# Attention scores spread over partitions by DMA transposes of 16-bit halves instead of TensorE transposes

## The chip, the cores and the metric

The kernel runs on one core of a Trainium2 chip. The metric is the device time of one execution in microseconds (us), lower is better. The engines are named as the profile names them: PE is the matrix engine (TensorE), PEld its weight loads, DVE the vector engine, ACT the scalar engine, POOL is GpSimd, SP the engine that issues DMAs.

## The reference, cut to what matters

There are 128 graphs of 128 nodes with 256 features, each with its own 128x128 matrix of edges. Layer 0 is a gated graph network: three rounds, each of which sums messages over the edges and puts them through a gated recurrent cell. Layer 1 is an attention over the edges, and this is where the change lies:

```python
h = jnp.maximum(_layernorm(x, axis=-1), 0.0)
Wh = jnp.einsum('bnf,fo->bno', h, W)
s = Wh.sum(axis=-1)
e = jax.nn.leaky_relu(s[:, :, None] + s[:, None, :], negative_slope=ALPHA)
e = jnp.where(adj == 0, -jnp.inf, e)
alpha = jax.nn.softmax(e, axis=-1)
h_prime = jnp.einsum('bpq,bqo->bpo', alpha, Wh)
x = x + h_prime
```

The score s is one number for each node. The sum `s[:, :, None] + s[:, None, :]` needs it twice: once by row and once by column.

## The kernel before, in words

The 128 graphs are worked on in 32 groups of four (`G`). A group's tiles hold the nodes of a graph on the 128 partitions, or its features, with the four graphs side by side.

Each group goes through three rounds of the gated cell (`gru` twice, then `gru_rows`, which leaves the nodes on the partitions) and then through `attention`. Rounds of different groups alternate: in the steady part the order is round 0 of group g, round 1 of g-1, round 2 of g-2, and so on (`turns`). One such round is a slot.

The gate products of a round (`products`, L663 and L670 in the profile) are made with a seven-product scheme, and their banks of PSUM, the matrix engine's output memory, are `x`, `y` and `q`, each in a part for two gates (`_rz`) and one for the third (`_n`). After its sixth product the `y` bank is copied to SBUF by ACT (`put`, L702 and L706) and then added to by the seventh product. PE's next products for `y_rz` must therefore wait for that copy; the products for `y_n` lie between. The remaining PE work of a group is: edge sums (L605), weighted sums of attention (L619), rows products of attention (L966), and the transposes of the scores (L923). They share two PSUM banks named `misc`.

The order of all instructions on every engine is written out by a planner, the class `Plan`. Every operation is given to it with an engine, a length in ns, and the buffers that it reads and writes. `run` plays the engines forward in time, with lags between engines (`LAG`: 250 to 300 ns, 4000 for a DMA), and at each step takes among the operations that can start first the one with the earliest rank. A rank is a due time less the lengths of what follows. The gate products are a chain of fixed order, one behind the other. Whatever feeds them is ranked earlier by `MARGIN`, which is 8000 ns before and 7000 after. Each engine then runs its list strictly in that order and waits on semaphores.

In `attention` (L891) the rows x1 are normalised to h1 (`normed`), of which there is one buffer. Then:

- Four DVE operations (L899) multiply h1 by the column sums of W and add up each row: the scores s, one column for each of the four graphs, a node on each partition.
- L917 makes e, which is 0 on edges and a huge negative number elsewhere.
- L923 spreads s over the partitions: for each graph, one column of s is read as a 128x128 tile (the column repeated 128 times) and PE transposes that. The result in `misc` has s of all nodes along the free dimension on every partition.
- L929 adds it to e, L930 adds s by row, L932 applies the leaky slope, L934 and L936 find the row maximum, L941 takes the exponential on ACT. The exponential is held back by `turn` until a given copy of a later group's round 1 has been made.
- e is transposed to eT. In all groups but the last two, `turned_weights` (L978) does this by DMA. A DMA transpose takes 16-bit elements, so ACT first splits e into a plane of low and one of high halves (`pe`, L985), SP issues one DMA transpose (L986) to `peT`, and ACT joins the halves again (L989). In the last two groups PE transposes e (L953) and ACT copies it (L955).
- `weighted` (L611) multiplies h1 by eT, L966 multiplies the result by W, L971 divides by the row sums and adds to x1, and x1 goes out.

The same DMA route by halves serves the states of the gated cell (`turned_halves`, L544 for the split, L554 for the DMA, L548 for the join).

Buffers are counted in the table `BUFS`. pe, peT, eT and h1 have one buffer, e and s two, `misc` two.

Of the kernel before, what the change touches and what calls it, by code (L numbers as in the profile page):

```python
# [11 lines left out]
U16 = mybir.dt.uint16  # L12
AF = mybir.ActivationFunctionType
OP = mybir.AluOpType
AX = mybir.AxisListType

P = 128
G = 4
# [2 lines left out]
SETS = 4  # L21
EARLY = 3
SLOT = 18150
MARGIN = 8000
GATES = 18150
BIG = 3.0e38

# [9 lines left out]
class Plan:  # L37
# [14 lines left out]
    def buf(self, tag):  # L52
        n, kind = self.tags[tag]
        if kind == "free" or kind == "turn":
            b = Buf(tag, tag, None)
            if kind == "turn":
                self.waiting.setdefault(tag, []).append((self.phase, len(self.waiting.get(tag, ())), b))
            return b
        key = (tag, self.group % SETS if kind == "set" else 0)
        uses = self.last.setdefault(key, [])  # L60
        b = Buf(tag, key, uses[-n] if len(uses) >= n else None)
        b.slot = (key[1], len(uses) % n)
        uses.append(b)
        return b
# [39 lines left out]
    def run(self):  # L104
# [29 lines left out]
        def rank_all():  # L134
            for i in reversed(topo):
                eng, ns, due = nodes[i][0], nodes[i][1], nodes[i][5]
                gap = 0 if i in bound else MARGIN
                rank[i] = min([due] + [rank[u] - (0 if nodes[u][0] == eng != "SP" else nodes[i][7])
# [72 lines left out]
def kernel(  # L211
# [21 lines left out]
    nc = tc.nc  # L233
    B, N, D = x.shape
    L = weight.shape[0]
    KD = D // P
    NG = B // G
# [5 lines left out]
    work = ctx.enter_context(tc.tile_pool(name="work", bufs=1))  # L243
# [5 lines left out]
        "at": (1, "all", work, [P, G, N]), "a": (6, "all", work, [P, G, N]),  # L249
        "hT": (1, "set", work, [P, KD, GN]), "rows": (3, "turn", work, [P, G, D]),  # L250
        "pl": (1, "turn", work, [P, 2, 3, GN]), "plT": (1, "turn", work, [P, 2, 3, GN]),
        "pe": (1, "all", work, [P, 2, G * N]), "peT": (1, "all", work, [P, 2, G * N]),
        "r1": (1, "turn", work, [P, G, D]), "p3": (1, "turn", work, [P, G, D]),
        "hs": (2, "turn", work, [P, 4, H]), "aT": (2, "turn", work, [P, KD, GN]),
        "gs": (2, "turn", work, [P, 4, H]),
# [35 lines left out]
    def ap(b):  # L291
        return phys[(b.tag,) + b.slot]

    plan = Plan({t: v[:2] for t, v in BUFS.items()})
    op, buf = plan.op, plan.buf

    ident = const.tile([P, P], F32, name="ident")
# [210 lines left out]
    def flat(b):  # L508
        return ap(b).rearrange("p q n -> p (q n)")
# [101 lines left out]
    def weighted(m, a, dst, lo, hi):  # L611

        n, cols = hi - lo, slice(lo * N, hi * N)
        for k in range(KD):
            ps = buf("misc")

            def sums(k=k, ps=ps):
                for b in range(lo, hi):
                    nc.tensor.matmul(flat(ps)[:, b * N:(b + 1) * N],  # L619
                                     ap(m)[:, b, k * P:(k + 1) * P], ap(a)[:, b, :],  # L620
                                     start=True, stop=True)
            op("PE", 225 * n, sums, [(m, lo, hi), (a, lo, hi)], [ps], [dst])
            units = (dst, 2 * k, 2 * k + 2) if n == G else (dst, 2 * k + lo // 2, 2 * k + hi // 2)
            op("ACT", 190 + 100 * n, lambda k=k, ps=ps: nc.scalar.copy(  # L624
                ap(dst)[:, k, cols], flat(ps)[:, cols]), [ps], [units])
# [224 lines left out]
    def group(g):  # L850
# [37 lines left out]
        for lo, hi in ((0, G),) if g < NG - 1 else ((G // 2, G), (0, G // 2)):  # L888
            attention(g, a, x1, h1, lo, hi)

    def attention(g, a, x1, h1, lo, hi):  # L891

        part, n = slice(lo, hi), hi - lo
        w1, w1_sum = W["w1"], W["w1_sum"]
        normed(x1, h1, lo, hi)
        s = buf("s")
        for b in range(lo, hi):
            hw = buf("hw")
            op("DVE", 520, lambda b=b, hw=hw: nc.vector.scalar_tensor_tensor(  # L899
                ap(hw), ap(h1)[:, b, :], 1.0, ap(w1_sum), op0=OP.mult, op1=OP.mult,  # L900
                accum_out=ap(s)[:, b:b + 1]), [(h1, b, b + 1), w1_sum], [hw, (s, b, b + 1)],
               two=True)

        e, top, low, den, rden = (buf(t) for t in ("e", "top", "low", "den", "rden"))

        def wide(t):
            return ap(t)[:, part, None].to_broadcast([P, n, N])

        def es():
            return ap(e)[:, part]

        def small(t):
            return ap(t)[:, part]
        cost = 155 + 134 * n
        op("DVE", 150 + 66 * n, lambda: nc.vector.tensor_scalar(  # L917
            es(), ap(a)[:, part], 0.0, -BIG, op0=OP.is_equal, op1=OP.mult), [(a, lo, hi)], [e])
        s_all = buf("misc")

        def turn_s():
            for b in range(lo, hi):
                nc.tensor.transpose(flat(s_all)[:, b * N:(b + 1) * N],  # L923
                                    ap(s)[:, b:b + 1].to_broadcast([P, P]), ident)

        def spread():
            return flat(s_all)[:, lo * N:hi * N].rearrange("p (b n) -> p b n", n=N)
        op("PE", 110 * n, turn_s, [s], [s_all], [e])
        op("DVE", cost, lambda: nc.vector.tensor_tensor(es(), es(), spread(), OP.add), [s_all], [e])  # L929
        op("DVE", cost, lambda: nc.vector.tensor_tensor(es(), es(), wide(s), OP.add), [s], [e],  # L930
           two=True)
        op("DVE", cost, lambda: nc.vector.scalar_tensor_tensor(  # L932
            es(), es(), ALPHA, es(), op0=OP.mult, op1=OP.max), [], [e], two=True)
        op("DVE", cost, lambda: nc.vector.tensor_reduce(small(top), es(), AX.X, OP.max),  # L934
           [e], [top])
        op("DVE", 150, lambda: nc.vector.tensor_scalar(  # L936
            small(low), small(top), -BIG / 1e3, -1.0, op0=OP.max, op1=OP.mult), [top], [low])

        def exps():
            for b in range(lo, hi):  # L940
                nc.scalar.activation(ap(e)[:, b, :], ap(e)[:, b, :], AF.Exp, bias=ap(low)[:, b:b + 1])  # L941
        op("ACT", 320 * n, exps, [low], [e], turn=(g + 2, 1, "rz"))
        op("DVE", cost, lambda: nc.vector.tensor_reduce(small(den), es(), AX.X, OP.add), [e], [den])
        op("DVE", 170, lambda: nc.vector.reciprocal(small(rden), small(den)), [den], [rden])
        eT, uT = buf("eT"), buf("uT")
        if g < NG - 2:
            turned_weights(e, eT)
        else:
            p_e = buf("misc")

            def turn():
                for b in range(lo, hi):
                    nc.tensor.transpose(flat(p_e)[:, b * N:(b + 1) * N], ap(e)[:, b, :], ident)  # L953
            op("PE", 110 * n, turn, [e], [p_e], [eT])
            op("ACT", 190 + 100 * n, lambda: nc.scalar.copy(  # L955
                ap(eT)[:, part].rearrange("p b n -> p (b n)"), flat(p_e)[:, lo * N:hi * N]),
               [p_e], [(eT, lo, hi)])

        weighted(h1, eT, uT, lo, hi)
        for m in range(lo, hi, 2):  # L960
            ps = buf("misc")

            def rows_product(m=m, ps=ps):
                for b in range(2):
                    for k in range(KD):
                        nc.tensor.matmul(ap(ps)[:, b, :], ap(uT)[:, k, (m + b) * N:(m + b + 1) * N],  # L966
                                         ap(w1)[:, k, :], start=(k == 0), stop=(k == KD - 1))
            op("PE", 4 * 432, rows_product,
               [(uT, m // 2, m // 2 + 1), (uT, 2 + m // 2, 3 + m // 2), w1], [ps])
            for b in range(2):  # L970
                op("DVE", 480, lambda b=b, i=m + b, ps=ps: nc.vector.scalar_tensor_tensor(  # L971
                    ap(x1)[:, i, :], ap(ps)[:, b, :], ap(rden)[:, i:i + 1], ap(x1)[:, i, :],
                    op0=OP.mult, op1=OP.add), [ps, rden], [(x1, m + b, m + b + 1)])
        op("SP", 100, lambda: nc.sync.dma_start(
            out[g * G + lo:g * G + hi].rearrange("b n d -> n b d"), ap(x1)[:, part]),
           [(x1, lo, hi)], [])

    def turned_weights(e, eT):  # L978

        pe, peT = buf("pe"), buf("peT")  # L980

        def halves(t):
            return ap(t).rearrange("p g n -> p (g n)").bitcast(U16).rearrange(
                "p (m two) -> p two m", two=2)
        op("ACT", 1045, lambda: nc.scalar.copy(ap(pe), halves(e)), [e], [pe])  # L985
        op("SP", 100, lambda: nc.sync.dma_start_transpose(  # L986
            ap(peT).rearrange("p two (g q) -> p (two g) q", q=P),
            ap(pe).rearrange("p two m -> p (two m)")), [pe], [peT])
        op("ACT", 1340, lambda: nc.scalar.copy(halves(eT), ap(peT)), [peT], [eT])  # L989

    weights()
    for g in range(NG):
# [33 lines left out]
```

## Time and profile before

The time is 2131.06 us, the median of three runs (2127.33 to 2132.03). The profiled execution spans 2129.0 us.

| engine | busy us | share |
|---|---|---|
| PE | 2108.4 | 99% |
| DVE | 1701.3 | 80% |
| ACT | 1536.5 | 72% |
| POOL | 923.8 | 43% |

| line | what | count | mean ns of one |
|---|---|---|---|
| L923 | PE transpose of s | 128 | 273 |
| L929 | DVE add of spread s, from PSUM | 31 of four graphs | 685 |
| L930 | DVE add of s by row, from SBUF | 31 of four graphs | 740 |
| L985 | ACT split of e | 30 | 1037 |
| L986 | DMA transpose pe to peT, issue to landing | 30 | 3.2 us |
| L989 | ACT join to eT | 30 | 1348 |
| L702 | ACT copies of gate banks | 448 | about 580 |

[...]What one adds to a full queue is seen from start to start. Idle time of an engine is put down to what released it. In the steady part the pattern repeats every two groups: the transposes of every second group start 129.20 us apart.

### The profile page before, as it was taken

Reading aid. Unit: us, or ns where it says so; the run is one execution under the profiler, and the core shown is the slowest. Engines: PE = TensorE matmul, PEld = TensorE weight load, DVE = VectorE, ACT = ScalarE, POOL = GpSimd, SP = SyncE. Lnnn points to the kernel's source line nnn. Section 1 sums busy time; section 2 is a strip of 40 time slices with the busy share of each in tenths; the row PEclk is TensorE's granted clock in tenths of the full one; section 3 lists DMA queues with packets and bytes.
Section 4 is the critical chain, followed back from the end, with each engine's and each line's share of the span. In section 5 each row is a group of like instructions: output and inputs, shape, how many; then the busy total and the mean of one; then the engine's idle time right before and its main releaser. Section 6 shows DMA issues by size and latency. Waiting matters only on the chain. (4 is left out here: it accounts for less than half of the span.)

```text
span 2129.0 us, 34073 instructions
## 1 busy us (share of the span) xinstructions
PE 2108.4 (99%) x12550; PEld 1882.8 (88%) x12550; DVE 1701.3 (80%) x3364; ACT 1536.5 (72%) x2771; POOL 923.8 (43%) x889
## 2 busy tenths in 40 slices
PE   8999999999999999999999999999999999999997
PEld 7888888898888998889998898998889988898896
DVE  7767898778787887877888787887878887877785
ACT  5567787767777676877767777677776777676663
POOL 5544454344543435434444443444434454434331
PEclk9999999999999999999999999999999999999997
DMA  4222223232222322323222322222223222212220
GB/s 144 45 50 50 48 51 72 50 65 54 64 67 55 79 56 50 68 58 80 45 60 58 75 67 50 65 56 64 66 55 75 60 50 70 60 31 53 58 75 30
DMA packets 333430, 129.35 MB, mean 61 GB/s; under 512 B 264656, under 2 KB 333008, under 8 KB 333264
## 3 DMA queue, kind: packets, MB, share of 16 engines
q1 hardware_dynamic: 333264, 127.18, 26.3%
q8 instruction: 98, 1.61, 0.3%
q14 instruction: 68, 0.56, 0.1%
HBM read 45.36 MB, written 16.78 MB: 29 GB/s over the span
## 5 line engine op out<-in xcount | busy, mean ns | idle before, releaser
L702 ACT COPY t_rz<-y_rz 128x512 f32<-128x512 f32 x192 | 112.3, 585 | 188.8 <-PE y_rz L663 114.3
L565 POOL TENSOR_TENSOR r<-rows 128x512 f32<-128x512 f32 x128 | 140.4, 1117 | 229.8 <-ACT rows L548 99.9
L712 DVE TENSOR_TENSOR t_rz<-t_rz,q_rz 128x512 f32<-128x512 f32 x192 | 131.3, 684 | 88.0 <-PE q_rz L663 40.4
L633 POOL TENSOR_TENSOR hs<-hT 128x512 f32<-128x512 f32 x96 | 131.8, 1373 | 156.3 <-PE y_n L670 72.4
L663 PE MATMUL y_rz<-hs,s_hh 128*128 128x256 f32 x768 | 197.4, 379 | 0.3 <-ACT t_rz L702 0.3
L663 PE MATMUL y_rz<-gs,s_x 128*128 128x256 f32 x768 | 197.1, 379 | 0.0
L663 PEld LDWEIGHTS y_rz<-gs,s_x 128*128 128x128 f32 x768 | 145.9, 190 | 19.8
L637 POOL TENSOR_TENSOR hs<-hT,hs 128x256 f32<-128x256 f32 x96 | 77.0, 802 | 198.1 <-PE q_n L670 160.4
L663 PEld LDWEIGHTS y_rz<-hs,s_hh 128*128 128x128 f32 x768 | 144.0, 190 | 20.1 <-issue 1.0
L590 POOL TENSOR_TENSOR pl<-d,pl 128x512 bf16<-128x512 f32 x64 | 80.8, 1264 | 185.1 <-ACT pl L588 184.9
L568 POOL TENSOR_TENSOR p<-r 128x512 bf16<-128x512 f32 x128 | 159.6, 1267 | 0.0
L712 DVE TENSOR_TENSOR t_n<-t_n,q_n 128x512 f32<-128x512 f32 x192 | 131.3, 684 | 26.4 <-PE q_n L670 12.6
L585 POOL TENSOR_TENSOR d<-hT,pl 128x512 f32<-128x512 f32 x64 | 77.6, 1214 | 139.2 <-DVE hT L791 65.2
L608 ACT COPY aT<-misc 128x512 f32<-128x512 f32 x192 | 112.0, 585 | 27.1 <-PE misc L605 23.3
L663 PE MATMUL x_rz<-hT,s_hh 128*128 128x256 f32 x512 | 131.5, 379 | 0.0
L663 PE MATMUL x_rz<-aT,s_x 128*128 128x256 f32 x512 | 131.4, 379 | 0.0
L966 PE MATMUL misc<-w,uT 128*128 128x256 f32 x512 | 125.5, 390 | 0.8 <-ACT uT L624 0.7
L829 POOL TENSOR_TENSOR x<-x,u 128x512 f32<-128x512 f32 x64 | 82.5, 1305 | 100.1 <-DMA x<-in_x_dram 54.9
L785 DVE TENSOR_TENSOR d<-hT,u 128x512 f32<-128x512 f32 x128 | 115.4, 901 | 10.5 <-ACT u L782 10.5
L663 PE MATMUL y_n<-hs,s_hh 128*128 128x256 f32 x384 | 114.3, 379 | 0.0
L663 PE MATMUL y_n<-gs,s_x 128*128 128x256 f32 x384 | 114.3, 379 | 0.0
L966 PEld LDWEIGHTS misc<-w,uT 128*128 128x128 f32 x512 | 98.6, 196 | 15.6 <-ACT uT L624 2.1
(219 smaller groups left out, 6418.5 us busy)
## 6 DMA issues: line engine op xcount, KB each, us to landing
rows<-in_x_dram SPq DMA_DIRECT2D x32, 512.0 KB, 4.2
x<-in_x_dram SPq DMA_DIRECT2D x32, 512.0 KB, 4.0
out_dram<-x SPq DMA_DIRECT2D x31, 512.0 KB, 2.9
at<-in_adj_dram SPq DMA_DIRECT2D x32, 256.0 KB, 2.8
plT<-pl SPq DMA_TRANSPOSE x186, 3.3
rz<-in_L_gnn_w_ih_dram SPq DMA_DIRECT2D x1, 768.0 KB, 5.0
rz<-in_L_gnn_w_hh_dram SPq DMA_DIRECT2D x1, 768.0 KB, 7.7
e<-in_L_gnn_weight_dram SPq DMA_DIRECT2D x3, 256.0 KB, 7.8
```

The costliest lines, as they stand in the source:

```text
L565: op("POOL", 1106, lambda part=part: nc.gpsimd.tensor_tensor(ap(r1)[:, part], ap(rows)[:, part], top(rows)[:, part], OP.subtract), [(rows, ...
L568: op("POOL", 1050, lambda part=part: nc.gpsimd.tensor_tensor(ap(p3)[:, part], ap(r1)[:, part], top(r1)[:, part], OP.subtract), [(r1, n, n ...
L585: op("POOL", 1150, lambda k=k, r=r: nc.gpsimd.tensor_tensor(ap(r), ap(hT)[:, k], part(pl, k, 0), OP.subtract), [(hT, 2 * k, 2 * k + 2), (p ...
L590: op("POOL", 1150, lambda k=k, r=r: nc.gpsimd.tensor_tensor(part(pl, k, 2), ap(r), part(pl, k, 1), OP.subtract), [r], [(pl, k, k + 1)])
L608: op("ACT", 590, lambda k=k, ps=ps: nc.scalar.copy(ap(dst)[:, k, :], flat(ps)), [ps], [(dst, 2 * k, 2 * k + 2)])
L633: op(eng, cost, lambda: sub(ap(w)[:, 0:2, :], blocks()[:, 1::2, :], blocks()[:, 0:2, :], OP.subtract), [t], [(w, 0, 2)], two=True)
L663: nc.tensor.matmul(ap(bank)[:, half, :], ap(w)[:, i - 1, q, :], source(t, sums), start=(first and c == 0 and m == 0), stop=False, skip_gro ...
L702: op("ACT", 590, lambda: nc.scalar.copy(ap(t), ap(y)), [y], [t], mark=mark)
L712: op("DVE", 690, lambda: nc.vector.tensor_tensor(ap(t), ap(t), ap(q), OP.add), [q], [t])
L785: op("DVE", 690, lambda j=j, d=d, cols=cols: nc.vector.tensor_tensor(ap(d), ap(hT)[:, j, :], ap(u)[:, cols], OP.subtract), [(hT, lo, hi), ...
L829: op("POOL", 1290, lambda cols=cols, part=part: nc.gpsimd.tensor_tensor(part(x1), part(x1), ap(u)[:, cols], OP.add), [(u, lo, hi)], [(x1, ...
L966: nc.tensor.matmul(ap(ps)[:, b, :], ap(uT)[:, k, (m + b) * N:(m + b + 1) * N], ap(w1)[:, k, :], start=(k == 0), stop=(k == KD - 1))
```

## The change

In all groups but the last two, s is spread by the route that e already takes: ACT writes the low and high halves of s, each repeated 128 times along the free dimension, into `pe`; one DMA transposes the eight 128x128 blocks to `peT`; ACT joins them into a new SBUF tile `s_all`, which L929 adds to e in place of the PSUM tile. The function `turned_weights` becomes `turned_halves_of`, which takes the halves, the source and the destination, and is called for s and for e. The last two groups keep the PE transposes. The planner is told that the add now reads two SBUF tiles (`two`, which makes it keep such operations apart from GpSimd's). `MARGIN` goes from 8000 to 7000. The purpose is to take the transposes of s off PE.

```diff
-MARGIN = 8000
+MARGIN = 7000
...
-        "pe": (1, "all", work, [P, 2, G * N]), "peT": (1, "all", work, [P, 2, G * N]),
+        "pe": (1, "all", work, [P, 2, G, N]), "peT": (1, "all", work, [P, 2, G, N]),
+        "s_all": (1, "all", work, [P, G, N]),
...
-        s_all = buf("misc")
-
-        def turn_s():
-            for b in range(lo, hi):
-                nc.tensor.transpose(flat(s_all)[:, b * N:(b + 1) * N],
-                                    ap(s)[:, b:b + 1].to_broadcast([P, P]), ident)
-
-        def spread():
-            return flat(s_all)[:, lo * N:hi * N].rearrange("p (b n) -> p b n", n=N)
-        op("PE", 110 * n, turn_s, [s], [s_all], [e])
-        op("DVE", cost, lambda: nc.vector.tensor_tensor(es(), es(), spread(), OP.add), [s_all], [e])
+        if g < NG - 2:
+            s_all = buf("s_all")
+
+            def spread():
+                return ap(s_all)
+            turned_halves_of(lambda: ap(s).bitcast(U16).rearrange("p (g two) -> p two g", two=2)
+                             [:, :, :, None].to_broadcast([P, 2, G, N]), s, s_all)
+        else:
+            s_all = buf("misc")
+
+            def turn_s():
...
+            op("PE", 110 * n, turn_s, [s], [s_all], [e])
+        op("DVE", cost, lambda: nc.vector.tensor_tensor(es(), es(), spread(), OP.add), [s_all], [e],
+           two=g < NG - 2)
...
         if g < NG - 2:
-            turned_weights(e, eT)
+            turned_halves_of(lambda: halves_of_blocks(e), e, eT)
...
-    def turned_weights(e, eT):
+    def halves_of_blocks(t):
+        return ap(t).bitcast(U16).rearrange("p g (m two) -> p two g m", two=2)
+
+    def turned_halves_of(halves, src, dst):
 
         pe, peT = buf("pe"), buf("peT")
...
-        op("ACT", 1045, lambda: nc.scalar.copy(ap(pe), halves(e)), [e], [pe])
+        op("ACT", 1045, lambda: nc.scalar.copy(ap(pe), halves()), [src], [pe])
         op("SP", 100, lambda: nc.sync.dma_start_transpose(
...
-        op("ACT", 1340, lambda: nc.scalar.copy(halves(eT), ap(peT)), [peT], [eT])
+        op("ACT", 1340, lambda: nc.scalar.copy(halves_of_blocks(dst), ap(peT)), [peT], [dst])
```

More of the change, by code (lines that the diff above doesn't have):

```diff
@@ L918, in attention, with spread @@
             es(), ap(a)[:, part], 0.0, -BIG, op0=OP.is_equal, op1=OP.mult), [(a, lo, hi)], [e])
-        s_all = buf("misc")
-        def turn_s():
-            for b in range(lo, hi):
-                nc.tensor.transpose(flat(s_all)[:, b * N:(b + 1) * N],
-                                    ap(s)[:, b:b + 1].to_broadcast([P, P]), ident)
-        def spread():
-            return flat(s_all)[:, lo * N:hi * N].rearrange("p (b n) -> p b n", n=N)
-        op("PE", 110 * n, turn_s, [s], [s_all], [e])
-        op("DVE", cost, lambda: nc.vector.tensor_tensor(es(), es(), spread(), OP.add), [s_all], [e])
+        if g < NG - 2:
[7 more added lines that the diff above has]
+            def turn_s():
+                for b in range(lo, hi):
+                    nc.tensor.transpose(flat(s_all)[:, b * N:(b + 1) * N],
+                                        ap(s)[:, b:b + 1].to_broadcast([P, P]), ident)
+            def spread():
+                return flat(s_all)[:, lo * N:hi * N].rearrange("p (b n) -> p b n", n=N)
+            op("PE", 110 * n, turn_s, [s], [s_all], [e])
+        op("DVE", cost, lambda: nc.vector.tensor_tensor(es(), es(), spread(), OP.add), [s_all], [e],
+           two=g < NG - 2)
         op("DVE", cost, lambda: nc.vector.tensor_tensor(es(), es(), wide(s), OP.add), [s], [e],
@@ L976, in attention @@
            [(x1, lo, hi)], [])
-    def turned_weights(e, eT):
+    def halves_of_blocks(t):
+        return ap(t).bitcast(U16).rearrange("p g (m two) -> p two g m", two=2)
+    def turned_halves_of(halves, src, dst):
         pe, peT = buf("pe"), buf("peT")
[L982 to L985, printed above, removed]
+        op("ACT", 1045, lambda: nc.scalar.copy(ap(pe), halves()), [src], [pe])
         op("SP", 100, lambda: nc.sync.dma_start_transpose(
-            ap(peT).rearrange("p two (g q) -> p (two g) q", q=P),
-            ap(pe).rearrange("p two m -> p (two m)")), [pe], [peT])
-        op("ACT", 1340, lambda: nc.scalar.copy(halves(eT), ap(peT)), [peT], [eT])
+            ap(peT).rearrange("p two g q -> p (two g) q"),
+            ap(pe).rearrange("p two g m -> p (two g m)")), [pe], [peT])
+        op("ACT", 1340, lambda: nc.scalar.copy(halves_of_blocks(dst), ap(peT)), [peT], [dst])
     weights()
```

## The prediction

> **What bounds the kernel now.** I read the busy table of the page first, then the busy time by stage, then TensorE's (PE's) instructions in order of time, then the line of the removed transposes, and last the attention of one group on all engines.
>
> ```profile
> PE 2108.4 (99%) x12550; PEld 1882.8 (88%) x12550; DVE 1701.3 (80%) x3364; ACT 1536.5 (72%) x2771; POOL 923.8 (43%) x889
> PE   8999999999999999999999999999999999999997
> ```
>
> PE is busy in every slice. A busy share can hide slow matmuls, so I also took PE's work from start to start. A matmul of 256 columns takes 0.216 us of PE's queue (four start 0.86 us apart), one of 128 fp32 columns 0.111, a bf16 one 0.056. Counts times these prices give 2115 us of work; between 100 and 2000 us no stretch of a hundred us holds more time than its work. PE's recorded waits come to about 6 us in the first 200 us and 9 us in the last 90.
>
> ```profile
> 12.00:391.00 379.00, 375.93 (x2200) 329.52 (x2199) 303.39 (x567) 272.30 (x507) 190.52 (x183) 1.00 0.25 57
> 391.00:1625.00 1234.00, 1234.00 (x7411) 1107.86 (x7410) 999.02 (x1978) 917.87 (x1638) 535.07 (x516) 1.00 0.28 62
> 2096.00:2129.00 33.00, 22.46 (x76) 17.09 (x76) 17.21 (x53) 8.63 (x21) 2.32 (x5) 0.67 0.14 48
> ```
>
> The columns are stretch, length, then busy PE, weight load, VectorE (DVE), ScalarE (ACT), GpSimd, clock and DMA share. In the long middle PE is never idle and the granted clock is 1.00; DVE has 235 us to spare, ACT 316. Only the last 33 us are a chain. Work taken off PE's queue is therefore time, as long as nothing else starves PE.
>
> ```profile
> L923 PE MATMUL misc<-ident,s x128: 272/273/322, 204.8 to 2111.9; 128*128 128x128 f32 x128
> ```
>
> The 273 ns is the length of one with its drain. What it takes of the queue is read where it stands:
>
> ```profile
> 1036.70 0.61 PE L670 MATMUL y_n<-s_hh,hs 128*128 128x128 f32 x4
> 1037.14 0.61 PE L670 MATMUL y_n<-s_x,gs 128*128 128x128 f32 x4
> 1037.59 0.60 PE L923 MATMUL misc<-ident,s 128*128 128x128 f32 x4
> 1038.03 1.03 PE L670 MATMUL y_rz<-s_hh,hs 128*128 128x256 f32 x4
> ...
> 1036.95 0.59 ACT L702 COPY t_rz<-y_rz 128x512 f32<-128x512 f32 x1 [1.66 <-PE y_rz L670]
> ```
>
> Four transposes hold the queue from 1037.59 to 1038.03, 0.44 us, not 4 x 0.273. The same lines show what they may do besides. The next y_rz product adds into the bank that ACT copies at that moment (1036.95 to 1037.54). The y_n products before it cover the copy by only 0.05 us; the transposes give PE something to do there. I call this place the seam. In PE's order 14 of the 33 groups of transposes stand in a seam alone or with others; rows products (L966, 1.72 us) or weighted sums (L619, 0.89 us) fill nearly all the rest.
>
> **What the Trainium skill says.** "Perfetto Trace Analysis", Identifying the Most-Contended Engine: matmul busy share is no good measure for TensorE, the weight loads' share is better. The trace agrees that both are high (99% and 88%), and the spacing above settles it. "TensorE: Matmul & The Clock Gate", Part 4: a PE transpose takes about 275 ns in a kernel's context and lands in PSUM. The trace has 273 ns, but in a full queue it costs 111 ns. "DMA: Bandwidth & Descriptors", DMA Transpose (X-bar): 2-byte elements only, into SBUF. That is why fp32 scores must be split into halves by a copy and put together by another; the kernel already does so for its weights e. "SBUF — State Buffer", Who interferes with whom: a two-input VectorE operation with both inputs in SBUF contends with GpSimd's reads. The trace agrees in size: the add from PSUM (L929) averages 685 ns, the one from SBUF (L930) 740.
>
> **The change, part by part.** It concerns 30 of the 32 groups.
>
> Removed from PE: 4 transposes a group, 30 x 0.444 = 13.3 us, all on the queue that sets the end. Also removed: one use a group of the two misc PSUM banks, which all of PE's side work shares. I give that nothing, since PE does not wait for banks in the middle.
>
> Laid bare on PE: up to 13 seams that only the transposes filled. A seam without filler shows what it costs: of the five in the trace, two (near 164 and 184 us) lengthen the following product from 1.03 to about 1.12 us, the others not. Lower bound: 0, because there are four rows products and four weighted sums for six seams in two groups, and another takes the place. Upper bound with a prompt ACT: 13 x 0.1 = 1.3 us. I take 1.3.
>
> Added to ACT: the split, priced by L985 at 1.04 us, and the join, by L989 at 1.35 us: 30 x 2.39 = 72 us. ACT goes from 72% to some 76%. ACT mostly waits for PE's products (187 us before the copies of L702 alone), so this lies in idle time. The danger is place, not sum: a 1.35 us copy that ACT has begun when PE reaches a seam holds back the eviction that PE needs. Four such copies a group (L544, L548) and the pair of e already run without PE waiting, because the order is planned with their lengths. I take 0; the other bound is under the rivals.
>
> Added to SP: 30 DMA transposes, each 1.23 us of SP's queue and 3.2 us to landing, priced by L986. Behind a waiting one on SP's queue stand the transposes of later layers (L554), loads and the output; those are issued many us ahead, and SP has long free stretches. The DMA share is 0.28. Nothing.
>
> Added to DVE: the add now reads SBUF, 685 to 740 ns, 30 x 0.055 = 1.7 us on an engine with 20% idle. Nothing.
>
> Lengthened: from scores to the spread scores it was 0.9 us from transposes to add. The same DMA route for e takes this long now, from the split's start to the join's end:
>
> ```profile
> 988.14 1.03 ACT L985 COPY pe<-e 128x1024 uint16<-128x1024 uint16 x1
> ...
> 995.65 1.35 ACT L989 COPY eT<-peT 128x1024 uint16<-128x1024 uint16 x1
> ...
> 1016.14 1.05 PE L619 MATMUL misc<-eT,h 128*128 128x128 f32 x8
> ```
>
> That is 8.9 us (the next group 9.2; the parts without queueing 1.04 + 3.2 + 1.35 = 5.6). So the chain grows by 5 to 8 us. Here eT is ready at 997.0 and first read at 1016.1, 19 us later; in the next group it is ready at 1054.8 and read at 1096, 41 us later. The lengthening fits in the smaller slack twice. h1, of which there is one buffer, is held until the weighted sums are done, but those come when PE's order puts them, not when eT is ready. The single pe and peT are now used twice in 64.6 us a group, for under 10 us each.
>
> MARGIN falls from 8000 to 7000: feeders of the gate products are preferred 1 us later, so the whole order is planned anew. The trace can't price that; I take 0, and between -3 and +3 us from the end part, which is a chain and not full.
>
> Sum: 2131.1 - 13.3 + 1.3 = **2119 us**.
>
> **The rivals.** (a) The seams open and ACT is late in them: each of the 13 then loses about 1 us (a 1.04 us split just begun, less 0.05 of cover): 2131 - 13 + 13 = **2131**, no change. For it: 13 transposes stand exactly there, and ACT gets two more long copies a group. Against: fillers outnumber seams.
> (b) The new copies or the longer chain make PE wait in every group, by a long copy, 1.0 to 1.3 us: 30 to 39 us given up for 13 gained, **2148** to 2157, slower. For it: ACT's copies are the tight return path to PE, cover 0.05 us in a seam, and a new order can be worse everywhere, since the steady part repeats. Against: not one such stall in 2,000 us with the six long copies that are there.
> (c) The third group from the end, the last to use DMA, finishes some 8 us later and stretches the closing chain: 2119 + 8 = **2127**. For it: the last 33 us are a chain. Against: its weights were split at 2063, with PE still full of gates until about 2090.
>
> **How the numbers follow.** Forecast 0.72, (a) 0.10, (b) 0.14, (c) 0.04. Low end: all 13.3 us, no open seam, 3 us better at the end and 2 us of spread between runs, 2113. The high end takes in (a) and (c) and the light side of (b), 2138. Faster by over 0.2% (under 2126.8): 0.73, the forecast and a little of (c). Within: 0.11, (a) and the rest of (c). Slower: 0.16, (b) and the bad side of (a).
>
> **What would show it.** Right: no PE transposes of s but 8 in the last two groups, 60 DMA transposes of pe, two groups in 128.3 us of the steady part in place of 129.20, PE busy throughout, ACT near 1608 us. Seams: rows products or weighted sums between y_n and the next y_rz. Wrong: PE waits for L702's copies in the steady part (rival a or b), with a split or join just ahead of the copy on ACT; or two groups over 129.2 us apart; or a last stretch after the gates longer than 33 us (c).

## The result, and the profile after

The changed kernel takes 2119.19 us (median of four runs, 2114.66 to 2121.44), the kernel before in the same comparison 2129.59 us. The ratio is 0.9948 with a 95% interval of 0.9927 to 0.9969: faster by 0.5%.

First the engines of the changed kernel, from the page, and its PE in 40 slices:

```profile
PE 2095.0 (99%) x12430; PEld 1868.1 (88%) x12430; DVE 1673.8 (79%) x3364; ACT 1589.5 (75%) x2831; POOL 945.9 (45%) x889
PE   8999999999999999999999999999999999999997
```

PE has 120 matmuls fewer, four in each of 30 groups, and is still busy everywhere. ACT has grown by 53 us of busy time. The stages follow: stretch, length, then busy PE, weight loads, DVE, ACT and GpSimd, the granted clock, the DMA share and GB/s (the last stretch begins where PE's gate work is nearly done):

```profile
12.00:391.00 379.00, 373.99 (x2175) 326.52 (x2175) 300.39 (x561) 275.55 (x510) 194.06 (x183) 1.00 0.27 59
391.00:1625.00 1234.00, 1234.00 (x7404) 1107.77 (x7403) 985.05 (x2000) 958.22 (x1691) 558.34 (x516) 1.00 0.30 66
2087.00:2119.70 32.70, 20.49 (x76) 15.38 (x76) 18.29 (x54) 8.77 (x21) 3.40 (x5) 0.76 0.15 49
```

The middle is as full as it was. What has changed there is the period: the products that follow a seam come back every 64.14 us a group, before every 64.60. The 0.46 us are the four transposes (0.444). Only eight PE transposes of s are left, and the DMA transposes of pe are 60:

```profile
L932 PE MATMUL misc<-ident,s x8: 272/273/323, 2081.5 to 2102.9; 128*128 128x128 f32 x8
...
peT<-pe SPq DMA_TRANSPOSE x60, 3.1
```

The seams are filled by other work. In PE's order of time in the changed kernel, a weighted sum stands between y_n and the next y_rz, and nothing is lost:

```profile
1013.40 0.59 PE L664 MATMUL y_n<-gs,s_x 128*128 128x256 f32 x2
1013.83 1.05 PE L620 MATMUL misc<-eT,h 128*128 128x128 f32 x8
1014.72 1.03 PE L664 MATMUL y_rz<-hs,s_hh 128*128 128x256 f32 x4
```

There were 13 seams with transposes alone in them and five bare ones; now 7 of the 96 are bare. Two of these cost something, near 206 and 2048 us. PE and then ACT near the first:

```profile
206.09 0.61 PE L671 MATMUL y_n<-s_x,gs 128*128 128x128 f32 x4
208.07 1.13 PE L671 MATMUL y_rz<-s_hh,hs 128*128 128x256 f32 x4 [1.37 <-ACT t_rz L703]
```

```profile
206.49 1.05 ACT L994 COPY pe<-s 128x1024 uint16<-128x1024 uint16 x1 [0.75 <-DVE hw L900]
207.44 0.58 ACT L703 COPY t_rz<-y_rz 128x512 f32<-128x512 f32 x1
```

ACT takes its list in order. The new split of s stands ahead of the copy that PE needs, and waits 0.75 us for the last score. So PE waits 1.37 us. The other wait, 1.48 us, stands behind the four operations of ACT that make h1. They are not new, and they come late because ACT waits 5.48 us for DVE:

```profile
2047.11 2.08 ACT L505 ACTIVATE h<-x,nm,rs 128x256 f32<-128x256 f32 x4 [5.48 <-DVE nm L501]
2049.10 0.57 ACT L703 COPY t_rz<-y_rz 128x512 f32<-128x512 f32 x1
```

For comparing kernels I use the time from the first of the 96 seams to the last. It is 2046.5 us before and 2036.0 after. The difference, 10.5, is about the 13.3 of transposes less 2.9 of these two waits. Smaller waits moved as well (near 200 us one of 1.2 us before, of 0.4 after), so that the sum fits this well is in part chance.

### The profile page after: what moved, and what is told of

Same layout as the page of the kernel before. It is cut to its first block, busy times and chain, and to the rows that moved or that the text cites. A ratio compares the mean times of both kernels' runs of the same rounds, so it can differ in the third digit from the quotient of the medians.

```text
span 2119.7 us, 33949 instructions
## 1 busy us (share of the span) xinstructions
PE 2095.0 (99%) x12430; PEld 1868.1 (88%) x12430; DVE 1673.8 (79%) x3364; ACT 1589.5 (75%) x2831; POOL 945.9 (45%) x889
## 5 line engine op out<-in xcount | busy, mean ns | idle before, releaser
L591 POOL TENSOR_TENSOR pl<-d,pl 128x512 bf16<-128x512 f32 x64 | 74.8, 1172 | 296.4 <-ACT pl L589 296.2
L638 POOL TENSOR_TENSOR hs<-hT,hs 128x256 f32<-128x256 f32 x96 | 82.4, 859 | 243.8 <-PE q_n L671 172.6
L634 POOL TENSOR_TENSOR hs<-hT 128x512 f32<-128x512 f32 x96 | 130.4, 1359 | 98.5 <-ACT hT L549 32.1
L569 POOL TENSOR_TENSOR p<-r 128x512 bf16<-128x512 f32 x128 | 155.1, 1232 | 0.0
L489 DVE BATCH_NORM_STATS2 st<-rows 128x6 f32<-128x256 f32 x128 | 45.2, 414 | 100.2 <-DMA rows<-in_x_dram 100.1
L609 ACT COPY aT<-misc 128x512 f32<-128x512 f32 x192 | 111.9, 585 | 15.2 <-PE misc L606 11.1
L786 DVE TENSOR_TENSOR d<-hT,u 128x512 f32<-128x512 f32 x128 | 109.8, 858 | 10.9 <-ACT u L783 10.8
L586 POOL TENSOR_TENSOR d<-hT,pl 128x512 f32<-128x512 f32 x64 | 91.3, 1428 | 45.4 <-ACT pl L584 39.6
```

Of the source, the lines that this page charges most:

```text
L569: op("POOL", 1050, lambda part=part: nc.gpsimd.tensor_tensor(ap(p3)[:, part], ap(r1)[:, part], top(r1)[:, part], OP.subtract), [(r1, n, n ...
L586: op("POOL", 1150, lambda k=k, r=r: nc.gpsimd.tensor_tensor(ap(r), ap(hT)[:, k], part(pl, k, 0), OP.subtract), [(hT, 2 * k, 2 * k + 2), (p ...
L609: op("ACT", 590, lambda k=k, ps=ps: nc.scalar.copy(ap(dst)[:, k, :], flat(ps)), [ps], [(dst, 2 * k, 2 * k + 2)])
L634: op(eng, cost, lambda: sub(ap(w)[:, 0:2, :], blocks()[:, 1::2, :], blocks()[:, 0:2, :], OP.subtract), [t], [(w, 0, 2)], two=True)
L638: op(eng, half, lambda: sub(ap(w)[:, 3, :], blocks()[:, 2, :], ap(w)[:, 2, :], OP.subtract), [t, (w, 2, 3)], [(w, 3, 4)], two=True)
L786: op("DVE", 690, lambda j=j, d=d, cols=cols: nc.vector.tensor_tensor(ap(d), ap(hT)[:, j, :], ap(u)[:, cols], OP.subtract), [(hT, lo, hi), ...
```

## The experiments

All times are medians. The ratio is that to the kernel before, run beside them, with its 95% interval; it is taken over all runs and so is not quite the quotient of two medians. The kernel before stood at 2128.7 to 2129.6 us beside the different sets. "Period" is us per group in the steady part, "seam to seam" the time from the first seam to the last, both from the profile of one execution.

| kernel | us | ratio | period | seam to seam |
|---|---|---|---|---|
| before | 2129.6 | 1 | 64.60 | 2046.5 |
| after (MARGIN 7000) | 2119.2 | 0.9948 (0.9927 to 0.9969) | 64.14 | 2036.0 |
| after, run again | 2118.3 | 0.9951 (0.9938 to 0.9965) | 64.14 | 2036.0 |
| after, MARGIN 8000 | 2134.5 | 1.0027 (1.0016 to 1.0038) | 64.65 | 2048.4 |
| before, MARGIN 7000 | 2128.1 | 0.9997 (0.9989 to 1.0005) | 64.61 | 2045.6 |
| no spread of s, 7000 | 2123.8 | 0.9972 (0.9961 to 0.9983) | 64.19 | 2040.3 |
| no spread of s, 8000 | 2120.4 | 0.9957 (0.9945 to 0.9970) | 64.16 | 2038.5 |
| after, PE transposes too | 2133.1 | 1.0023 (1.0015 to 1.0030) | 64.57 | 2049.0 |
| after, ACT copies twice | 2120.8 | 0.9961 (0.9949 to 0.9974) | 64.14 | 2038.3 |
| 8000, one copy moved | 2125.0 | 0.9982 (0.9975 to 0.9990) | 64.14 | 2040.3 |
| after, MARGIN 6000 | 2120.2 | 0.9962 (0.9950 to 0.9975) | 64.14 | 2031.3 |
| after, MARGIN 5000 | 2116.9 | 0.9942 (0.9929 to 0.9956) | 64.14 | 2032.3 |
| after, two swaps on ACT | 2118.6 | 0.9950 (0.9937 to 0.9962) | 64.14 | 2034.0 |
| MARGIN 5000, three swaps | 2113.9 | 0.9937 (0.9924 to 0.9949) | 64.14 | 2031.3 |

The order of "before, MARGIN 7000" repeats only every six groups, and its period is the mean of six. Every edit that changes the list of operations makes the planner write a new order, so each row is one order, not one isolated cost.

**The transposes given back.**

```diff
+            idle = buf("misc")
...
+            op("PE", 110 * n, turn_idle, [s], [idle])
```

> The changed kernel with the four PE transposes of s still made in each of the 30 groups, into a bank that nobody reads. Theory: 30 x 0.444 = 13.3 us return, 2130 to 2134, and the steady part goes back from 64.15 to 64.60 us a group. Rival (the transposes only filled places where PE would have waited anyway): 2119 to 2122.

2133.1 us and a period of 64.57: the 13.9 us to the changed kernel are the transposes' own time and a little more. They were work on a full queue, not the filling of gaps. The run gives back their use of the misc banks as well; but PE waits for no bank in the middle of this kernel or of the changed one, and the transposes' own time accounts for the sum.

**The two edits apart.**

```diff
-MARGIN = 7000
+MARGIN = 8000
```

> The changed kernel with MARGIN back at 8000, all else as changed. Theory (the time follows the work on PE's full queue): 13.3 us less PE work than before, so 2116 to 2121; if the 2.5 us that the changed kernel is late in its first 32 us come from MARGIN, 2117, else 2119. Rival (the new order that MARGIN gives is what brings the gain): back near 2129.

> The kernel before with MARGIN 7000, transposes on PE as before. Theory: PE's work is unchanged, so 2128 to 2132, or 2 to 3 us above before if the late start of the changed kernel comes from MARGIN. Rival (the gain is MARGIN's): about 2119.

The second came as the theory had it: the new MARGIN alone changes nothing in the time. The first did not. With MARGIN 8000 the change makes the kernel slower, 2134.5 us, though PE has the same 13.3 us less to do. Neither theory nor rival had that. The list of PE's waits shows what is new (who waits for whom, us in total, times, longest):

```profile
PE misc L620 <- ACT aT L609: 6.4, 21, 0.8
```

The weighted sum waits for a bank of misc, once in every group of the steady part, until ACT has copied the edge sums out of it. Here is one of the 21 in PE's and ACT's order at MARGIN 8000:

```profile
1032.56 1.08 PE L671 MATMUL q_rz<-s_hh,hs 128*128 128x256 f32 x4
1033.89 1.16 PE L620 MATMUL misc<-eT,h 128*128 128x128 f32 x8 [0.25 <-ACT aT L609]
```

```profile
1029.92 0.72 ACT L783 ACTIVATE u<-u,bias_i 128x512 f32<-128x512 f32 x1 [2.33 <-DVE u L774]
1030.55 0.49 ACT L777 ACTIVATE rz<-t_rz,bias_s 128x256 f32<-128x256 f32 x1
1030.95 0.57 ACT L696 COPY q_rz<-seed_q 128x512 f32<-128x512 f32 x1
1031.46 0.50 ACT L759 ACTIVATE rz<-t_rz,bias_s 128x256 f32<-128x256 f32 x1
1031.87 0.57 ACT L696 COPY q_n<-seed_q 128x512 f32<-128x512 f32 x1
1032.39 0.53 ACT L703 COPY y_rz<-x_rz 128x512 f32<-128x512 f32 x1
1032.86 0.51 ACT L777 ACTIVATE rz<-t_rz,bias_s 128x256 f32<-128x256 f32 x1
1033.27 0.57 ACT L609 COPY aT<-misc 128x512 f32<-128x512 f32 x1
```

The q_rz products end their turn at 1033.42 (four times 0.216 after 1032.56) and the sum starts at 1033.89, so 0.47 us are lost, of which the record gives 0.25 as waiting. ACT is late because it waited 2.33 us for a DVE operation, and then works off the seven operations that stand ahead of the copy. That operation is the last DVE line here. It is late for a reason that DVE's own order shows, with GpSimd's beside it:

```profile
1025.43 1.51 DVE L792 SCALAR_TENSOR_TENSOR hT<-d,u 128x512 f32<-128x512 f32 x1
1026.86 0.94 DVE L770 SCALAR_TENSOR_TENSOR u<-rz,t_n 128x256 f32<-128x256 f32 x1
1027.84 1.26 DVE L774 SCALAR_TENSOR_TENSOR u<-u,t_n 128x256 f32<-128x256 f32 x1
...
1029.47 0.42 DVE L774 SCALAR_TENSOR_TENSOR u<-u,y_n 128x256 f32<-128x256 f32 x1
```

```profile
1025.23 1.16 POOL L591 TENSOR_TENSOR pl<-d,pl 128x512 bf16<-128x512 f32 x1 [1.66 <-ACT pl L589]
1026.35 1.18 POOL L638 TENSOR_TENSOR hs<-hT,hs 128x256 f32<-128x256 f32 x1
1027.67 1.15 POOL L586 TENSOR_TENSOR d<-hT,pl 128x512 f32<-128x512 f32 x1
```

The first three of these DVE operations take 0.69, 0.42 and 0.42 us elsewhere in that order. They are stretched while three GpSimd operations run one behind the other. The Trainium skill, "SBUF — State Buffer", Who interferes with whom, says that a DVE operation with two SBUF inputs contends with a GpSimd operation that reads SBUF; the lines agree, 2.2 us of delay in three operations. The whole trace agrees too: where GpSimd is idle none of the three takes over 0.70 us, and the form of L774 that takes y_n from PSUM stays at 0.42 us whether GpSimd works beside it or not. That this stretch is the first cause of PE's wait is read from the trace and was not tried. It is not enough for the wait: in the run that follows, the same three operations are stretched to the same 1.51, 0.94 and 1.26 us, ACT waits the same 2.33 us, and PE doesn't wait.

**The wait at 8000 taken away.** In the order planned at MARGIN 8000 the one copy (L609 of round 0) goes two places forward on ACT; all other engines keep their lists.

```diff
+            if k == 0 and turns[plan.phase][1] == 0:
+                ahead.append(len(plan.nodes))
...
+        for i in ahead:
+            at = order.index(i)
+            for _ in range(2):
...
+                order.insert(to, order.pop(at))
```

> The changed kernel at MARGIN 8000 with one edit to ACT's order alone: the first copy of the edge sums of round 0 goes two places forward, ahead of a gate copy and a tanh; every other engine's order is as in the run at MARGIN 8000. Theory (the loss at 8000 is one wait a group, of a weighted sum for the misc bank that this copy holds, 0.47 us with the switch): the wait goes, 64.65 falls to about 64.2 us a group from slot 21 to 80, and 2134.5 to about 2125. Rival (the loss at 8000 is spread over the order): 2133 to 2136.

2125.0 us, period 64.14. With the copy at 1031.38 the sum follows the q_rz products without a wait:

```profile
1031.55 1.08 PE L674 MATMUL q_rz<-s_hh,hs 128*128 128x256 f32 x4
1032.47 1.05 PE L623 MATMUL misc<-eT,h 128*128 128x128 f32 x8
```

The sum now starts 0.92 us after the first of the four q_rz products and not 1.33, and holds the queue for 0.89 us and not 0.99; together that is the 0.51 us by which the periods differ. So two places in one engine's list decide over 9.5 us. The 6 us that still part it from the changed kernel are single waits: 2.3 us near 200, 1.7 near 247, and 5.7 in the last 40 us, where the changed kernel has 0.4, none and 2.7.

**What the DMA route costs.**

```diff
-            s_all = buf("s_all")
+            s_all = s
...
-                return ap(s_all)
-            turned_halves_of(...)
+                return wide(s)
```

> The changed kernel (MARGIN 7000) with neither PE transposes nor the DMA route for s in the 30 groups: the add takes the scores by row a second time, so the sum s[q] is left out of e and s[p] counted twice. It tells what the route by ACT, SP and DMA costs. Theory: the 72 us of ACT copies and the longer chain lie in idle time but for the two PE waits of 1.4 and 1.5 us, so 2115 to 2119. Rival (ACT's copies delay PE in many places and eat part of the gain): 2109 or less.

> At MARGIN 8000, neither PE transposes nor the DMA route for s in the 30 groups (s[p] counted twice, s[q] left out of e). Theory A (the loss at 8000 comes from the route: its ACT copies and longer chain crowd the edge sums' copy): no recurring wait, about 64.15 us a group and 2117 to 2121. Theory B (any order planned without the four transposes at 8000 has its own accidents, the route's copies are not the cause): a recurring wait remains, 2125 or above.

At 8000 the recurring wait is gone without the route, as theory A had it: the order with the route has the wait and the order without it has not. Which part of the route does it, ACT's copies or the longer chain, is not shown, since both left together. But leaving the route out does not make the kernel faster than the changed one. At 7000 it is even 4.6 us slower, and my expectation of 2115 to 2119 missed. Its profile shows two losses near 210 us that the changed kernel does not have: y_n waits 3.0 us for its copy, which ACT has behind an exponential, and then the matmuls run at half their rate:

```profile
211.69 0.71 PE L671 MATMUL y_n<-s_hh,hs 128*128 128x128 f32 x4 [3.01 <-ACT t_n L703]
...
212.69 1.82 PE L671 MATMUL x_rz<-s_hh,hT 128*128 128x256 f32 x4
214.30 1.91 PE L671 MATMUL x_rz<-s_x,aT 128*128 128x256 f32 x4
```

Four matmuls of 256 columns take 1.6 to 1.7 us from start to start here, elsewhere 0.86, and the granted clock is 0.50 from 212.8 to 216.2 us. That is another 1.6 us in this execution; the six runs of this kernel lie between 2119.5 and 2125.0. The order without the route at 8000 has a wait of the same kind there, 1.9 us, without the drop of the clock. Of the two single waits of the changed kernel the one near 206 us shrinks to 0.2, and the one near 2048 stays, 1.47 us: the route is not its cause. Both periods are about those of the changed kernel. The route of 30 times 2.4 us costs PE nothing in the steady part.

```diff
+        for _ in range(2 if src.tag == "s" else 1):
             op("ACT", 1045, lambda: nc.scalar.copy(ap(pe), halves()), [src], [pe])
```

> The changed kernel with the split and the join of s each made twice in the 30 groups: another 72 us on ACT, which goes to some 79% busy. Theory (ACT's sum is not the limit, only a copy in the wrong place costs): the steady part stays near 64.15 us a group, 2117 to 2124 in all. Rival (ACT is near its limit, and its copies already cost PE): 1 us or more in each group, 2150 or above.

(The join is doubled in the same way.) 2120.8 us and a period of 64.14 with ACT at 78%. In the middle stage ACT is now at 1000.68 of 1234 us:

```profile
391.00:1625.00 1234.00, 1233.97 (x7404) 1107.54 (x7404) 1015.87 (x1998) 1000.68 (x1731) 562.53 (x517) 1.00 0.30 66
```

ACT's sum is not a limit here.

**MARGIN, and the two single waits.**

> The changed kernel with MARGIN 5000. Theory (7000 is one good order among many; the gain of 13 us is there wherever PE has no recurring wait): between 2117 and 2126, and the steady part either 64.15 us a group or longer by the length of a recurring wait. Rival (lower MARGIN is better in itself, since work that is not on the chain comes earlier): below 2117.

> The changed kernel with MARGIN 6000, for which the planner's own end is 9 us later than at 7000 and 4 us later than at 8000. Theory (PE work is the floor, and each order adds its own waits): 2122 to 2136, and if the steady part is over 64.15 us a group, one recurring wait of PE makes up the difference. Rival (any MARGIN up to 7000 is good for the changed kernel): 2116 to 2121.

The edit is the number alone. 5000, 6000 and 7000 share the period of 64.14; of those tried only 8000 has the recurring wait. At 5000, 2116.9 us lies on the line between theory and rival. The steady part is the theory's; that a lower MARGIN is better in itself is neither shown nor excluded, for 6000 is no better than 7000 in time, and both lower ones are 4 to 5 us shorter from seam to seam. At 6000 I expected too much, 2122 or more: its waits of 5.3 and 3.7 us stand in the closing chain alone. The planner's own end had put 6000 behind 8000, and on the chip it is 14 us ahead, so the planner's end did not tell which of these orders is good.

```diff
...
+                if order[to] not in behind or plan.nodes[i][3] & set(order[to:at]):
+                    break
+                order.insert(to, order.pop(at))
...
```

Here `ahead` holds the copies of y_rz to t2_rz, `behind` the splits of s and the h1 operations.

> The changed kernel once more, unedited, as the measure for the others of this set. Both theories: 2117 to 2121. What is open is its start: the profile of it lost 2.5 us between 24 and 32 us at a granted clock of 0.79. If that belongs to the execution and not to the order, this profile may have 1.00 there.

> The changed kernel with two swaps in ACT's order and no other: the copy of y_rz that PE waits for near 206 us goes ahead of the split of s, the one near 2048 us ahead of the last of the four h1 operations. Theory (these two waits of 1.4 and 1.5 us are ACT copies in the wrong place): the first wait goes, the second shrinks by half a us, about 2 us less than the changed kernel beside it. Rival (PE would wait there anyway, for the seam is bare): no difference, and the wait near 206 us still over 1 us.

> MARGIN 5000 with the same kind of swap, which it meets in three places (near 200 us, one later in the first part, and near 2042 us). The run at 5000 had waits of 0.96 and 0.25 us there. Theory: about 1 us less than at 5000, 2114 to 2118, with the steady part at 64.14 us a group; 3 us below the changed kernel beside it. Rival (the 5000 result was a good draw): 2118 to 2121.

With the first swap the seam near 206 us closes (y_n at 205.89, y_rz at 206.34) and with the second the wait near 2048 falls from 1.48 to 0.98. Seam to seam it is 2034.0 against 2036.0, the 2 us expected. In the run times this does not show: 2118.6 against 2118.3 beside it. Three swaps at 5000 take 0.9 us off seam to seam against 5000 alone, and give the lowest time here, 2113.9. It is faster than before; its interval overlaps that of the changed kernel beside it (0.9951), so that it beats the changed kernel is likely and not shown.

## Why the prediction was right, and where it was not

**The time** was forecast at 2119 and is 2119.2. That the two agree to 0.2 us is luck in part: the forecast took 12 us off 2131.1, and beside the changed kernel the one before ran at 2129.6, so that the gain is 10.4 us. By steps:

- PE's full queue: right, though a sum is wrong. Counts times prices give 2083 us and not 2115, and PE's waits in the first 200 us come to 7.7 us and not 6. In every hundred us between 200 and 2000 the priced work is still over 99% of the time, so the reading stands.
- The 13.3 us of transposes: right. The period falls by 0.46 us a group, and they come back when the transposes do.
- Seams laid bare: the mechanism right in part, the size off. I took 13 x 0.1 = 1.3 us. (Of the five bare seams before, three lengthen the next product, not two: the one near 2060 us as well.) In the steady part no seam is bare, since rows products and weighted sums took the places: the lower bound of 0 held there. Two seams at the edges lose 1.4 and 1.5 us, each by an ACT operation ahead of the eviction (the copy that frees the bank). The first stands behind the new split, as rival (a) had it for 13, and one swap on ACT removed it. The second stands behind h1 operations and is there without the route too.
- ACT's 72 us at nothing, by their sum: shown, by the period with all of them twice. ACT's busy time was forecast near 1608 us and is 1589.5: neighbouring operations overlap in the record (the split at 1035.13 lasts 1.05 us, the next operation starts 0.95 us after it), and busy time counts the overlap once.
- The longer chain at nothing: right. In the changed kernel one group's s goes from the split at 1035.13 to the end of the join at 1041.67, 6.5 us; eT is ready at 1059.0 and first read at 1078.0, again 19 us later.
- MARGIN at nothing, within 3 us: this step failed, without harm to the sum. It is right for the kernel before (0.9997), and I had looked at it as an edit for itself. Together with the removal it decides: 15.4 us lie between 7000 and 8000, and at 8000 the change is a loss. That is rival (b) in kind, a wait in every group by a late ACT copy, though at a bank of misc and not in a seam, and some 0.5 us long, not 1.0 to 1.3. I had found no such wait in the old order and took this for a property of the kernel. It was one of the order. Nothing in the trace before could tell that the order at 7000 would be free of it; here the forecast had luck.
- Rival (c) did not come: the part behind the gates is no longer than before (36.9 us after the last gate product, before 38.4, both with the clock down for part of it), and PE's waits in it are the same ones as before, the longest 2.65 and 1.78 us.

So the forecast was right for its main reason, but it claimed more certainty than it had a right to. Without knowing the new order, 0.14 for a recurring wait was low: one of the four values of MARGIN that were tried has one.

## What to carry to other kernels

Where one engine's queue is full, work taken off it is worth its spacing in the queue, from one start to the next (here 111 ns a transpose, not the 273 ns that the record gives as its length), provided the order leaves it fed. With an order planned by a model, an edit and a planner's constant are one change: measure both, and look first for a wait that comes back in every period, for here half a us in each of some 20 groups outweighed every single wait at the edges. It was cured by moving one instruction in the late engine's list.

## What the runs showed of the hardware

Two profiles of the same changed kernel differ by 6.4 us in span (2119.7 and 2113.2), and not at all from the first seam to the last (2036.0 in both). All of it lies at the edges, where PE has waits: 2.1 us before the first seam, 4.3 after the last. From 24 to 32 us, in the first profile and in the second:

```profile
24.00:32.00 8.00, 6.32 (x22) 4.55 (x21) 7.83 (x13) 5.15 (x12) 4.39 (x4) 0.79 0.41 132
```

```profile
24.00:32.00 8.00, 6.56 (x36) 5.46 (x35) 7.83 (x13) 5.76 (x14) 4.81 (x5) 1.00 0.39 132
```

The column before the DMA share is the granted clock, 0.79 and 1.00; the counts in brackets are matmuls, 22 and 36. In the first, the clock is 0.50 from 28.7 to 32.1 us, at the end of a wait of PE of 1.44 us for DVE, and matmuls of 256 columns start 0.43 us apart in place of 0.216; the second had the same wait and kept its clock. So the late start of the first profile, 2.5 us, is not in every execution of this order; what decides it is not shown. In the closing part, from 2080 to 2099 us, the clocks are 0.77 and 1.00. Differences of 2 to 6 us between single runs of one order can thus come from the clock alone, and one of 2 us between two orders is better read from seam to seam than from the run times, as long as the clock stays at 1.00 between the seams. In the run without the route at MARGIN 7000 it did not.
